# Projecting queries and keys together with the values, and turning them on VectorE and through DRAM

## The chip, the cores and the metric

The kernel runs on one core of a Trainium2 chip. The metric is the device time of one execution in microseconds (us). TensorE (PE) multiplies matrices; its weight loads have a row of their own in the profile (PEld). VectorE (DVE) and ScalarE (ACT) work on tiles element by element, GpSimd (POOL) and SyncE (SP) mostly issue transfers here. Matrix products land in PSUM, eight banks of 512 fp32 numbers on each of 128 partitions; everything else on the chip lies in SBUF.

## The reference

The input x has 4 images of 64 channels and 96 x 96 positions. Two layers follow one another, each on a group-normalized input and each added to what it got. The first is an attention with a sigmoid in place of a softmax; it takes nearly all of the time. The second filters a few frequencies of a 2-D Fourier transform.

```python
def _L0_conv_ref(x, wq, bq, wk, bk, wv, bv, ca_w1, ca_w2):
    q = jnp.einsum('bchw,oc->bohw', x, wq) + bq[None, :, None, None]   # 8 rows
    k = jnp.einsum('bchw,oc->bohw', x, wk) + bk[None, :, None, None]   # 8 rows
    v = jnp.einsum('bchw,oc->bohw', x, wv) + bv[None, :, None, None]   # 64 rows
    energy = jnp.einsum('bcn,bcm->bnm', Q, K)                          # 9216 x 9216
    att = jax.nn.sigmoid(energy)
    out = jnp.einsum('bcm,bnm->bcn', V, att).reshape(B, C, H, W) + x
    ...
    return out * scale[:, :, None, None]

x = x + _L0_conv_ref(_gn(x), ...)
x = x + _L1_conv_ref(_gn(x), ...)
```

## The kernel before

Two images make a pair and fill the 128 partitions; pair 0 runs through the attention first, then pair 1. The 9216 queries of a pair are cut into 18 blocks of 512, its keys into 72 pieces of 128. A tile is the product of 128 keys of one image with the 512 queries of a block: 144 tiles for each block of a pair, 5184 in all.

Tiles are worked in bursts of up to seven, one PSUM bank each. The eighth bank holds the block's sum (the accumulator, bank 7 or bank 0 by turns). In a burst, `energies` (L481) makes the tiles, with keys as the stationary and queries as the moving operand; `sigmoids` (L500) turns them into `at` in two ACT instructions, one over the first HEAD = 3 banks and one over the rest; `attend` (L517) multiplies values with `at` of the burst before and adds to the accumulator. While ACT works on burst t + 1, TensorE attends burst t. Queries and keys have 8 rows for each image. They are held four times over, as high and low parts of the fp32 numbers, so that a product over 32 rows of the faster fp32r form gives the accuracy of fp32.

Projections are steps between these. `keys` (L423 to L432) projects 512 positions with two matmuls of 256 columns; VectorE then adds the bias (L406), rounds to the high part (L407) and forms the low or high part (L416) in `kT`. `values_of` (L434 to L445) takes eight matmuls of 128 columns (L439), with x stationary, and one VectorE evacuation (L443) into `vT`. `queries` (L447 to L463) takes two matmuls of 256 columns (L452) and then eight VectorE instructions (L406, L407, twice L416, four times L462).

The order on TensorE, ACT and VectorE is written out by a planning loop (L671 to L737). It fills `together` (steps of a burst that use a bank of the next burst once the sigmoid has read it), `alone` (a step that takes the place of a tile: such a burst has six), and `ends` (work on VectorE or transfers after a burst). `done` (L733) says up to where a burst attends. A burst whose attention runs into the next block is a crossing; at the crossing the accumulator changes banks. During pair 0's first block its 18 pieces of keys and values are made just ahead of their use; pair 1's replace them while pair 0's last block runs. Queries of a block are made AHEAD = 42 tiles before it. In pair 1's time the second layer of pair 0 runs in the gaps. `halves` (L401) and `low_or_high` (L414) are the helpers of the splits.

The transfers on SP and POOL keep the order that the framework's scheduler gives them; each waits for what it needs, and holds up those behind it on its own queue.

Of the kernel before, what the change touches and what calls it, by code (L numbers as in the profile page):

```python
# [53 lines left out]

SIZE, HEAD = 7, 3
AHEAD = 6 * SIZE
ALL = NPAIR * NBLK * TILES
# [12 lines left out]

FIRST = {"wq": P, "wk": P, "wv": P, "pav": P, "bq": 1, "bk": 1, "low": 2, "nhalf": 1, "bv": P}
SECOND = {"w1": 2 * R, "w2": P, "ident": P, "fw": 2 * KW, "fh": 4 * KH, "gh": 2 * H, "gw": 4 * W}
# [11 lines left out]
def tile_kernel(ctx: ExitStack, tc: tile.TileContext, x, cst, late, spec, out):  # L84
# [299 lines left out]
    with tc.tile_pool(name="work", bufs=1) as work, \  # L384
# [10 lines left out]

        kT = kvp.tile([P, NCH // 2, P], F32R, tag="kT", name="kT")

# [3 lines left out]
        def halves(src, bias, name):  # L401

            shape = [P, src.shape[-1]]
            u = qp.tile(shape, F32, tag="full", name=f"full_{name}", bufs=1)
            h = qp.tile(shape, F32R, tag="high", name=f"high_{name}")
            nc.vector.tensor_scalar(u, src, bias, None, ALU.add)  # L406
            nc.vector.tensor_copy(h, u)  # L407
            return u, h
# [14 lines left out]
        def keys(p, s):  # L423
            pp = bank_a(f"pk_{p}_{s}")
            src = xs[p][:, bass.ts(s, NB)].rearrange("p (a e m) -> p e a m", e=2, m=P)
            for e in range(2):
                cols = bass.ts(e, P // 2)
                projected[0] = nc.tensor.matmul(pp[cols, :NB // 2], named("wk")[:, cols],  # L428
                                                src[:, e, :, :], start=True, stop=True)
            ku, kh = halves(pp[:, :NB // 2], named("bk"), f"k_{p}_{s}")  # L430
            low_or_high(kT[:, 2 * s:2 * s + 2, :].rearrange("p a m -> p (a m)"), ku, kh,
                        low_sb[:, 1:2])  # L432

        def values_of(p, s):  # L434
            pp = bank_a(f"pv_{p}_{s}")

            for i in range(4):
                for e in range(2):
                    projected[0] = nc.tensor.matmul(  # L439
                        pp[bass.ts(e, P // 2), bass.ts(i, P)],  # L440
                        xs[p][:, bass.ts(2 * (4 * s + i) + e, P // 2)], named("wv"),
                        start=True, stop=True)
            nc.vector.tensor_tensor(  # L443
                vT[:, 4 * s:4 * s + 4, :], pp.rearrange("p (i m) -> p i m", m=P),
                named("bv").unsqueeze(1).to_broadcast([P, 4, P]), ALU.add)  # L445

        def queries(p, n):  # L447
            pq = bank_a(f"pq_{p}_{n}")
            half = NB // 2
            for e in range(2):  # L450
                rows = bass.ts(e, P // 2)
                projected[0] = nc.tensor.matmul(  # L452
                    pq[rows, :half], named("wq")[:, rows],
                    xs[p][:, n * NB + e * half:n * NB + (e + 1) * half], start=True, stop=True)
            qu, qh = halves(pq[:, :half], named("bq"), f"q_{p}_{n}")
            q = qp.tile([P, NB], F32R, tag="q", name=f"q_{p}_{n}")
            for e in range(2):
                rows, cols = bass.ts(e, P // 2), bass.ts(e, half)
                low_or_high(q[rows, cols], qu[rows, :], qh[rows, :], low_sb[rows, 0:1])
                for b in range(2):  # L460
                    to, of = 64 * (1 - e) + 32 * b, 64 * e + 32 * b
                    nc.vector.tensor_copy(q[to:to + 32, cols], q[of:of + 32, cols])  # L462
            return q  # L463
# [13 lines left out]
        def energies(t):  # L477

            for i in range(total[t] - sizes[t], total[t]):
                r = 32 * (i % 4)  # L480
                nc.tensor.matmul(banks[:, bank_of(i), :], kT[r:r + 32, i // 4 % (NCH // 2), :],  # L481
                                 ask[i // TILES][r:r + 32, :], start=True, stop=True)
# [4 lines left out]
        def parts(t):  # L487

            for lo, part in ((0, order[t][:HEAD]), (HEAD, order[t][HEAD:])):
                if part:  # L490
                    yield 7 * (t % 2) + lo, min(part), len(part)
# [93 lines left out]
        norm0[0]()  # L585
        norm0[1]()
        keys(0, 0)
        warm_behind()
        q = first_queries()
        warm_behind()  # L590
        values_of(0, 0)
        warm_behind()
# [74 lines left out]
        kept = [TILES * (NPAIR * NBLK - 1) + 2 * (STRIP // P) * (s + 1) for s in range(NSTRIP)]  # L667
        ask, asked, known, valued, renewed, again_at = {0: q}, 1, 2, 2, 0, 0
        sizes, total, order, done, block, edges = [6], [6], [list(range(1, 7))], [], [], set()
        way = 1  # L670
        while len(done) < len(sizes):  # L671

            t, was = len(done), done[-1] if done else 0
            n = max(1, -(-was // TILES))
            edge = TILES * n
            crossing = edge < ALL and edge < total[t] - 3
            block.append(n if crossing else n - 1)
# [12 lines left out]
            elif total[t] < ALL:  # L690
                steps = together.setdefault(t, [])
                while known < NBLK and known <= (total[t] + 2 * SIZE - 1) // 8:
                    steps.append(lambda s=known: keys(0, s))
                    if known + 1 < NBLK:
                        end(t, norm0[known + 1])
                    known += 1
                while valued < NBLK and valued <= (total[t] + 2 * SIZE - LAG) // 8:
                    steps.append(lambda s=valued: values_of(0, s))
                    valued += 1
                if renewed < NBLK and was >= TILES * (NBLK - 1) + 8 * (renewed + 1):  # L700
                    steps.append(lambda s=renewed: keys(1, s))
                    steps.append(lambda s=renewed: values_of(1, s))
                    renewed += 1
                if asked < NPAIR * NBLK and total[t] + AHEAD >= TILES * asked and t not in alone:
                    steps.append(lambda n=asked: ask.update({n: queries(n // NBLK, n % NBLK)}))
                    asked += 1
                assert len(steps) <= HEAD
                while chain and not steps and t not in alone:
                    own, step, wait, since = chain[0]
                    if t < max(ready[0] + wait, started[0] + since):  # L710
                        break
                    if own:
                        alone[t] = step
                    elif own is None:
                        end(t, step)
                    else:
                        steps.append(step)
                    ready[0] = t
                    chain.pop(0)
# [6 lines left out]
            if crossing:  # L726
                way = 1 if n % 2 else -1
            elif together.get(t - 1):
                way = -way
            order.append(list(free)[::way][:ALL - total[t]])  # L730
            sizes.append(len(order[-1]))
            total.append(total[t] + sizes[-1])
            done.append(total[-1] - LAG if crossing else min(edge, total[-1] - LAG))  # L733
            while again_at < NSTRIP and done[t] >= kept[again_at]:
# [9 lines left out]

        spare[0] = 0
        energies(0)
        sigmoids(0)
        later(norm0[2])
        keys(0, 1)
        warm_behind()  # L750
        values_of(0, 1)
        with tc.manual_schedule(engines=ENGINES):
            put_off = []
            for t in range(T):
# [9 lines left out]
                if t + 1 < T:  # L764
                    sigmoids(t + 1)
                at_work = next((i for i in range(old, len(items)) if sum(
                    c.stop - c.start for _, c in items[:i]) >= 2 * NB), len(items))
                attend(items[old:at_work])
                for i, step in enumerate(together.get(t, ())):
                    spare[0] = order[t + 1][i]  # L770
                    step()
# [192 lines left out]
def _constants(l0):  # L964
# [19 lines left out]
    for name, w, bias in (("wq", "wq", "bq"), ("wk", "wk", "bk")):  # L984
        for col in range(P):
            b, o = col // 32 % 2, col % C8
            a[b * C:(b + 1) * C, PLACE[name].start + col] = l0[w][o]
            a[col, PLACE[bias].start] = l0[bias][o]
    for b in range(2):
        rows = slice(b * C, (b + 1) * C)  # L990
        a[rows, PLACE["wv"].start + b * C:PLACE["wv"].start + (b + 1) * C] = l0["wv"].T
        a[rows, PLACE["w1"].start + b * R:PLACE["w1"].start + (b + 1) * R] = l0["ca_w1"].T
        a[b * R:(b + 1) * R, PLACE["w2"].start + b * C:PLACE["w2"].start + (b + 1) * C] = \
# [3 lines left out]

    put("low", -np.stack([row // 8 % 2, row // 16 % 2], 1))
    put("nhalf", -0.5)
# [47 lines left out]
```

## Time and profile before

| What | Value |
|---|---|
| Median of three runs | 3080.54 us (3079.90 to 3081.23) |
| The profiled execution | 3080.95 us, span of its instructions 3079.2 us |
| First energies | 26.4 us after the span's start |
| Last energies | 2989.1 us |
| Attention, L517 | 11824 matmul records, 2408.3 us busy |
| Energies, L481 (all blocks but the first) | 5040 matmuls, 544.7 us busy |
| Sigmoids, L500 | 1503 instructions, 2394.5 us busy |
| Values' projection, L439 | 576 records, 37.7 us busy |
| Keys' projection, L428 | 144 records, 22.3 us busy |
| Queries' projection, L452 | 140 records, 21.1 us busy |
| DMA in the attention of pair 0 | about 1 GB/s |

A matmul in fp32 leaves two records, one in the fp32r form one. Matmuls are pipelined and two or four of them run side by side in parts of the array, so that busy times of single records overlap; the time between the starts of the same line in successive bursts is the better measure of a burst. The chain of waits goes back from the last instruction to whatever released each one, and gives the share of the span that each line holds.

### The profile page before, as it was taken

The numbers are of one execution on the slowest core, as the hardware profiler recorded it, in microseconds if no ns is written. First come the engines' busy times: TensorE is split into PE (matmuls) and PEld (weight loads), VectorE is DVE, ScalarE is ACT, GpSimd is POOL, SyncE is SP. The second block draws the span as 40 slices with busy tenths as digits, with TensorE's granted clock in tenths as the row PEclk, the third lists the DMA queues.
The fourth block names the chain that finished last, engine by engine and source line by source line (L and its number), as shares of the span: only waits on it lengthen the run. The fifth ranks groups of instructions, "written<-read, shape, count | busy, mean of one in ns | idle before, by whom it ended". The sixth has DMA issues, their size and how long they took to land.

```text
span 3079.2 us, 42720 instructions
## 1 busy us (share of the span) xinstructions
PE 3055.0 (99%) x19022; PEld 1145.5 (37%) x19022; DVE 387.2 (13%) x818; ACT 2417.3 (79%) x1543; POOL 27.1 (1%) x52
## 2 busy tenths in 40 slices
PE   8999999999999999999999999999999999999998
PEld 4433333333333333334433333333333333333336
DVE  4300000000000000002312111100110000000005
ACT  4688888888888888887688887777777888888872
POOL 0000000000000000000000000000001000000001
PEclk9999999999999999999999999999999999999999
DMA  3000000000000000000122322412113000000027
GB/s 145 1 1 1 1 1 1 1 1 1 1 1 1 1 1 1 1 1 1 31 75 61 84 74 77 132 24 29 50 44 131 1 1 1 1 1 1 5 63 246
DMA packets 80490, 99.48 MB, mean 32 GB/s; under 512 B 48209, under 2 KB 58193, under 8 KB 80209
## 3 DMA queue, kind: packets, MB, share of 16 engines
q1 hardware_dynamic: 72000, 71.57, 8.0%
q0 software_dynamic: 5776, 20.45, 1.9%
q10 hardware_dynamic: 2528, 4.72, 0.4%
q8 instruction: 149, 2.44, 0.3%
q14 instruction: 37, 0.29, 0.0%
HBM read 67.49 MB, written 28.05 MB: 31 GB/s over the span
## 4 chain that ended last, share of the span: by engine, by line
PE 98%; DVE 1%; ACT 1%; DMA 0%; issue 0%; SPq 0%; DVEq 0%; ACTq 0%
PE banks L517 75%; PE banks L481 16%; PE banks L439 1%; PE banks L428 1%; PE banks L206 1%; PE banks L376 1%; ACT at L500 0%; PE banks L452 0%; PE py L955 0%; PE pv L206 0%; DMA x<-in_x_dram 0%; PE pa L857 0%; PE banks L354 0%; PE idle_I-15036_15051 L820 0%; PE pu L869 0%
## 5 line engine op out<-in xcount | busy, mean ns | idle before, releaser
L500 ACT ACTIVATE at<-banks 128x1536 f32<-128x1536 f32 x1503 | 2394.5, 1640 | 590.6 <-PE banks L481 564.3
L517 PE MATMUL banks<-at,vT 128*64 128x512 f32 (+1 forms) x11824 | 2408.3, 546 | 0.0
L517 PEld LDWEIGHTS banks<-at,vT 128*64 128x64 f32 x11824 | 780.3, 136 | 1338.6 <-issue 1280.1
L481 PE MATMUL banks<-q,kT 32*128 32x512 f32 x5040 | 544.7, 453 | 2.6 <-ACT at L500 2.5
L481 PEld LDWEIGHTS banks<-q,kT 32*128 32x128 f32 x5040 | 223.6, 183 | 453.8 <-ACT at L500 340.0
L406 DVE TENSOR_SCALAR full_q<-banks,cs 128x256 f32<-128x256 f32 x35 | 16.9, 483 | 1361.0 <-PE banks L452 1361.0
L523 DVE SCALAR_TENSOR_TENSOR x<-banks,x 128x512 f32<-128x512 f32 x36 | 24.9, 692 | 648.9 <-PE banks L517 648.9
L462 DVE CAST q<-q 32x256 fp32r<-32x256 f32 x140 | 39.9, 285 | 3.8
L439 PE MATMUL banks<-cs,x 128*64 128x128 f32 x576 | 37.7, 273 | 0.4 <-DVE at L471 0.4
L379 DVE TENSOR_TENSOR x<-banks,x 128x384 f32<-128x384 f32 x24 | 13.4, 558 | 188.0 <-PE banks L376 186.1
L439 PEld LDWEIGHTS banks<-cs,x 128*64 128x64 f32 x576 | 33.8, 137 | 7.3 <-issue 0.9
L416 DVE SCALAR_TENSOR_TENSOR q<-high_q,cs,full_q 64x256 fp32r<-64x256 f32 x70 | 33.6, 480 | 1.8
L406 DVE TENSOR_SCALAR full_k<-banks,cs 128x256 f32<-128x256 f32 x36 | 17.4, 484 | 115.6 <-PE banks L428 89.8
L443 DVE TENSOR_TENSOR vT<-banks,cs 128x512 f32<-128x512 f32 x36 | 24.7, 685 | 9.7 <-PE banks L439 9.7
L525 DVE TENSOR_REDUCE maxs<-x 128x1 f32<-128x512 f32 x36 | 24.7, 686 | 1.2
L619 DVE COPY ws<-banks 128x512 f32<-128x512 f32 x16 | 11.1, 692 | 95.7 <-PE banks L206 95.6
L531 DVE BATCH_NORM_STATS2 stats<-x 128x6 f32<-128x512 f32 x36 | 22.2, 680 | 6.0 <-DMA x<-in_x_dram 5.8
L428 PE MATMUL banks<-x,cs 128*64 128x256 f32 x144 | 22.3, 388 | 0.2 <-DVE x L152 0.2
L570 PE MATMUL banks<-x 128*128 128x256 f32 (+1 forms) x46 | 14.9, 470 | 6.3 <-DMA x<-in_x_dram 6.3
L452 PE MATMUL banks<-x,cs 128*64 128x256 f32 x140 | 21.1, 379 | 0.0
L481 PE MATMUL banks<-q_first,kT 32*128 32x512 f32 x144 | 17.1, 463 | 2.8 <-DVE kT L416 1.7
L376 PE MATMUL banks<-cs,ws 128*64 128x384 f32 x96 | 19.6, 486 | 0.0
(133 smaller groups left out, 467.8 us busy)
## 6 DMA issues: line engine op xcount, KB each, us to landing
ws<-in_spec_dram SPq DMA_DIRECT2D x20, 512.0 KB
x<-in_x_dram SPq DMA_DIRECT2D x14, 512.0 KB
room<-in_spec_dram SPq DMA_DIRECT2D x12, 512.0 KB
w<-in_spec_dram POOLq DMA_DIRECT2D x10, 512.0 KB, 6.8
old<-in_x_dram SPq DMA_DIRECT2D x12, 384.0 KB
x1d<-x SPq DMA_DIRECT2D x12, 384.0 KB
xd<-old SPq DMA_DIRECT2D x12, 384.0 KB
xT<-xd SPq DMA_DIRECT2D x36, 128.0 KB
```

Source lines behind the costliest of these rows:

```text
L206: self.last = nc.tensor.matmul(pv[bass.ts(g, 32), :].rearrange("q (n k o) -> q n k o", n=SIDE, o=C)[:, :, k, :], self.ut[:, at:at + 32], s ...
L376: nc.tensor.matmul(py[bass.ts(b, C), :4 * W], self.z[:, i, bass.ts(b, C)], named("gw"), start=True, stop=True)
L406: nc.vector.tensor_scalar(u, src, bias, None, ALU.add)
L416: mark[0] = nc.vector.scalar_tensor_tensor(dst, h.bitcast(F32), is_low, u, ALU.mult, ALU.add)
L428: projected[0] = nc.tensor.matmul(pp[cols, :NB // 2], named("wk")[:, cols], src[:, e, :, :], start=True, stop=True)
L439: projected[0] = nc.tensor.matmul(pp[bass.ts(e, P // 2), bass.ts(i, P)], xs[p][:, bass.ts(2 * (4 * s + i) + e, P // 2)], named("wv"), star ...
L443: nc.vector.tensor_tensor(vT[:, 4 * s:4 * s + 4, :], pp.rearrange("p (i m) -> p i m", m=P), named("bv").unsqueeze(1).to_broadcast([P, 4, P ...
L462: nc.vector.tensor_copy(q[to:to + 32, cols], q[of:of + 32, cols])
L481: nc.tensor.matmul(banks[:, bank_of(i), :], kT[r:r + 32, i // 4 % (NCH // 2), :], ask[i // TILES][r:r + 32, :], start=True, stop=True)
L500: nc.scalar.activation(at[:, of:of + n, :], banks[:, bank:bank + n, :], AF.Sigmoid)
L517: attended[0] = nc.tensor.matmul(acc[half, cols], vT[:, j, half], at[:, place(2 * pair + b), cols], start=(j == 0), stop=(j == NCH - 1 and ...
L523: nc.vector.scalar_tensor_tensor(blk, acc, 1.0, blk, ALU.mult, ALU.add, accum_out=sums[p][:, m:m + 1])
```

## The change

Queries and keys lose their own projections, but for the first pieces. The values' weights get 32 more columns (16 for each image of the pair: 8 of the queries, 8 of the keys), so `values_of` makes all three, transposed, over two PSUM banks. VectorE adds the biases, splits queries and keys into high and low parts while they have positions on partitions, and turns them with one transpose. Four transfers on SP write the result to a DRAM tensor `split`, 32 rows of the three kinds for each piece. From there `known_keys` reads a piece of keys with four transfers on POOL, and `queries` a block of queries with eight transfers on SP, each of whole rows of 512 numbers.

Keys of pair 0's first seven pieces are still projected directly (DIRECT = 7), as are the first block's queries. The values of the very first piece keep the width of 128.

The transpose leaves the positions of a piece in another order. Stationary operands are therefore read with a step of two numbers: x in the values' projection, and `kT` in `energies`. The pieces of `vT` follow in the same order.

The planner changes too. Values are made further ahead (four bursts' tiles instead of two, less the lag). A values step takes two banks, so a burst's head, which ACT reads first, grows where steps need more than three. The first burst has five tiles instead of six. The rule for `crossing` and `done` is new. Reads of queries go into `ends` and no longer take a step. The three projections ahead of the first burst get banks of their own.

```diff
+QK = 4 * C8
+DIRECT = 7
...
-            src = xs[p][:, bass.ts(s, NB)].rearrange("p (a e m) -> p e a m", e=2, m=P)
             for e in range(2):
                 cols = bass.ts(e, P // 2)
-                projected[0] = nc.tensor.matmul(pp[cols, :NB // 2], named("wk")[:, cols],
-                                                src[:, e, :, :], start=True, stop=True)
+                projected[0] = nc.tensor.matmul(
+                    pp[cols, :NB // 2], named("wk")[:, cols],
+                    xs[p][:, bass.ts(2 * s + e, NB // 2)], start=True, stop=True)
...
+        def values_of(p, s, width=P + QK):
+            pp = banks[:, spare[0]:spare[0] + 2, :2 * width].rearrange(
+                "p h (a m) -> p h a m", a=2)
+            src = xs[p][:, bass.ts(s, NB)].rearrange("p (a m h) -> p a h m", a=2, h=2)
+            for h in range(2):
+                for a in range(2):
+                    for e in range(2):
+                        projected[0] = nc.tensor.matmul(
+                            pp[bass.ts(e, P // 2), h, a, :], src[:, a, h, bass.ts(e, P // 2)],
+                            named("wv")[:, :width], start=True, stop=True)
...
+            u = qp.tile([P, 2, 2, QK], F32, tag="u", name=f"u_{p}_{s}", bufs=1)
+            t = qp.tile([P, 3, 2, 2, QK], F32R, tag="t", name=f"t_{p}_{s}", bufs=1)
             nc.vector.tensor_tensor(
+                u, pp[:, :, :, P:].rearrange("p h a m -> p a h m"),
+                named("bqk").unsqueeze(1).unsqueeze(1).to_broadcast([P, 2, 2, QK]), ALU.add)
+            values()
...
+            for whole, to in pieces:
+                nc.vector.tensor_copy(to[:, 0], whole)
+                nc.vector.tensor_tensor(to[:, 1], whole, to[:, 0].bitcast(F32), ALU.subtract)
+            turned = qp.tile([P, 3, 2, NB // 8], F32, tag="turned", name=f"turned_{p}_{s}")
+            nc.vector.transpose(turned.rearrange("p k a (m h) -> p (k a) h m", h=2),
+                                t.rearrange("p k a h m -> p (k a) h m").bitcast(F32))
+            for g in range(4):
+                nc.sync.dma_start(
+                    split[p][s].rearrange("r k (a g m) -> g r (k a) m", a=2, g=4)[g],
+                    turned[bass.ts(g, QK)].rearrange("r k a m -> r (k a) m"))
+
+        def known_keys(p, s):
+            for r in range(4):
+                nc.gpsimd.dma_start(
+                    kT[bass.ts(r, QK), s, :].bitcast(F32),
+                    split[p][s][:, r % 2, bass.ts(r // 2, NB // 2)])
 
         def queries(p, n):
...
             q = qp.tile([P, NB], F32R, tag="q", name=f"q_{p}_{n}")
+            for i in range(8):
+                nc.sync.dma_start(
+                    q[bass.ts(i, QK // 2), :].bitcast(F32),
+                    split[p][n][bass.ts(i // 2 % 2, QK // 2), 2, :])
             return q
...
-                nc.tensor.matmul(banks[:, bank_of(i), :], kT[r:r + 32, i // 4 % (NCH // 2), :],
+                nc.tensor.matmul(banks[:, bank_of(i), :],
+                                 kT[r:r + 32, i % TILES // 8, :].rearrange(
+                                     "r (m h) -> r h m", h=2)[:, i // 4 % 2],
                                  ask[i // TILES][r:r + 32, :], start=True, stop=True)
...
-            crossing = edge < ALL and edge < total[t] - 3
+            crossing = edge < min(ALL, total[t] - 1)
...
-                while known < NBLK and known <= (total[t] + 2 * SIZE - 1) // 8:
-                    steps.append(lambda s=known: keys(0, s))
+                if known < DIRECT and known <= (total[t] + 2 * SIZE - 1) // 8:
+                    steps.append((1, lambda s=known: keys(0, s)))
                     known += 1
-                while valued < NBLK and valued <= (total[t] + 2 * SIZE - LAG) // 8:
-                    steps.append(lambda s=valued: values_of(0, s))
+                while (valued < min(NBLK, (total[t] + 4 * SIZE - 1) // 8 + 1)
+                       and sum(n for n, _ in steps) <= 2):
+                    steps.append((2, lambda s=valued: values_of(0, s)))
+                    if valued >= DIRECT:
+                        end(t, lambda s=valued: known_keys(0, s))
                     valued += 1
...
                 if renewed < NBLK and was >= TILES * (NBLK - 1) + 8 * (renewed + 1):
-                    steps.append(lambda s=renewed: keys(1, s))
-                    steps.append(lambda s=renewed: values_of(1, s))
+                    steps.append((2, lambda s=renewed: values_of(1, s)))
+                    end(t, lambda s=renewed: known_keys(1, s))
                     renewed += 1
-                if asked < NPAIR * NBLK and total[t] + AHEAD >= TILES * asked and t not in alone:
-                    steps.append(lambda n=asked: ask.update({n: queries(n // NBLK, n % NBLK)}))
+                if asked < NPAIR * NBLK and total[t] + AHEAD >= TILES * asked:
+                    end(t, lambda n=asked: ask.update({n: queries(n // NBLK, n % NBLK)}))
                     asked += 1
...
-            done.append(total[-1] - LAG if crossing else min(edge, total[-1] - LAG))
+            to = was + sizes[-1]
+            if to > total[t] - to % 2:
+                to = max(total[-1] - LAG, min(to, total[t] - total[t] % 2))
+            done.append(max(edge + 2, to) if crossing else min(edge, to))
...
-        spare[0] = 0
         energies(0)
         sigmoids(0)
         later(norm0[2])
+        spare[0] = 7
         keys(0, 1)
-        warm_behind()
+        spare[0] = 0
         values_of(0, 1)
```

## The prediction

> **What bounds the kernel now.** I read the busy shares first, then the chain of waits, then the same chain in short windows, then the groups of instructions by shape.
>
> ```profile
> PE 3055.0 (99%) x19022; PEld 1145.5 (37%) x19022; DVE 387.2 (13%) x818; ACT 2417.3 (79%) x1543; POOL 27.1 (1%) x52
> PE banks L517 75%; PE banks L481 16%; PE banks L439 1%; PE banks L428 1%; PE banks L206 1%; PE banks L376 1%; ACT at L500 0%; PE banks L452 0%; PE py L955 0%; PE pv L206 0%; DMA x<-in_x_dram 0%; PE pa L857 0%; PE banks L354 0%; PE idle_I-15036_15051 L820 0%; PE pu L869 0%
> ```
>
> TensorE is 99% of the span and 98% of the chain. A busy share can hide stalls, so the windows decide (start, us, what):
>
> ```profile
> 345.66 0.67 PE banks L481 x7
> 346.33 2.30 PE banks L517 x12
> 348.62 0.43 PE banks L452 x4
> 349.06 0.86 PE banks L517 x4
> 349.92 0.67 PE banks L481 x6
> 350.58 3.16 PE banks L517 x16
> ...
> 1443.76 0.43 PE banks L428 x4
> 1444.19 0.87 PE banks L439 x16
> 1445.06 0.86 PE banks L517 x4
> 1445.92 0.86 PE banks L481 x5
> ```
>
> A plain burst of seven tiles is 0.67 of energies and 3.16 of attention, 3.82 us. The burst with queries is 0.67 + 2.30 + 0.43 + 0.86 = 4.26: the projection's 0.43 is added whole, nothing hides it. Keys add 0.43, values 0.87. The energies after such a burst took 0.86 instead of 0.67: VectorE had not emptied the values' bank, as it does the keys first. ScalarE needs 3.22 us of each burst, so it doesn't take over when TensorE sheds these additions. A second stall, where a block of 512 queries ends:
>
> ```profile
> 449.39 0.46 PE banks L481 x2
> ...
> 449.93 0.77 ACT at L500
> 450.69 0.58 issue
> 451.27 1.88 ACT at L500
> ```
>
> Here attention stopped at the block's end and all of the next burst's work belonged to the new block, whose sum's bank ScalarE was still reading; by starts of successive bursts, the pair took 2.96 + 4.94 us against 3.82 + 3.39 elsewhere.
>
> **What the skill says.** SBUF — State Buffer, Specifications: lines of 16 bytes, full bandwidth from two hits a line on. That bears on the new layout of kT and x, read as stationary operand with a step of two fp32, two hits a line. The trace agrees at the extremes: step 1 takes 183 ns, z at L955 with a step of 32 elements 306 ns, both 32x128:
>
> ```profile
> L481 PEld LDWEIGHTS banks<-q,kT 32*128 32x128 f32 x5040 | 223.6, 183 | 453.8 <-ACT at L500 340.0 <-issue 110.4 <-DVE x L165 0.8
> L955 PEld LDWEIGHTS py<-cs,z 32*128 32x128 f32 x192 | 14.2, 306 | 0.8 <-DVE z L943 0.8
> ```
>
> No run shows step two. The same page, SBUF: two separate sides, says that VectorE's two-port operations keep GpSimd from writing descriptors for DMAs issued there, which bears on the keys' reads; no run before shows such a collision. DMA: Bandwidth & Descriptors, Anatomy of one DMA, puts the fixed cost of a transfer at about 2 us; here small ones measured 2.5 to 2.9.
>
> **The change part by part.**
>
> *Queries' projection goes.* 35 times 0.43. One falls in the first block, laid out below; 34 x 0.431 = 14.7 us off the path. Their VectorE work (about 2.9 us each) lay beside TensorE and frees nothing. The eight reads on SP's queue are issued about a block ahead where the q buffer allows; SP's order puts each behind the release of that buffer and few waits. Even asked 42 tiles (six bursts, 23 us) ahead, eight issues of 0.33 to 0.45 and a landing of 2.6 take 6 us. Cost nothing; if SP were blocked longer than the cover, each block would wait.
>
> *Pair 1's keys go, values widen.* Eighteen bursts of keys and values alternate between 5.13 and 5.33 us, 1.39 above plain. Afterwards values have 160 moving columns instead of 128: 0.87 x 160/128 = 1.08 us, plus 0.07 where VectorE's evacuation runs long: 1.15. VectorE now takes the 128-wide queries and keys first (a fixed 0.18 and 1 ns an element, from 128x512 at 685 ns and 128x384 at 558 ns: 0.31), then values 0.69; the two banks are free 1.2 us after the last matmul, about when the next energies reach them. 18 x 0.24 = 4.3 us.
>
> *Block ends.* The rule for `done` now always lets an ending burst begin in the old block. Four pairs of bursts lose 0.69 and four 0.27 (7.475 against 7.21): 3.8 us.
>
> *The first block (31 bursts from the first energies).* Here the added waits sit. A widened projection takes VectorE 0.31 + 0.69, six splits of 64 elements at about 0.2 (a 128x1 subtraction takes 158 ns, and 64 more elements 0.07), a transpose of 384 at 0.55 (768 takes 945 ns), some 3.0 us with gaps; direct keys 1.3, a normalization 0.54. That is 4.9 of the 5.3 us of a burst with both, so it keeps up, but the burst with two values needs 7.1 in 6.3 and the start carries a backlog. Behind each chain on VectorE's queue wait the next keys, for which energies wait. I laid the bursts out one by one with these durations. The same sheet gives 165.9 us for the start of the 31st burst before, where the trace has 166.0. Afterwards:
> - Start: separate banks let the queries' projection go before the keys' evacuation: 0.35 sooner. Five tiles instead of six shorten the first interval to 2.9 (3.79 before), and cost 0.4 in the last burst.
> - Removed: 24.7 us of additions in bursts 1 to 20. Added: five keys with values at 1.51, one double at 2.16, nine values at 1.08, together 19.4.
> - New stalls: 1.6 us behind the second chain, 2.8 behind the double, as keys 5 come after two chains.
> - Keys of chunks 7 to 17 go through DRAM. Four writes of 0.45 issue each and 2.6 to land (a write issued on SP at 3044.59 was seen at 3047.07) are 4.1; four reads on POOL, 0.52 each with 2.6 to land, are 4.2. In all 8.3 us after the transpose. From transpose to need there are two bursts, 10.2 less a spill of 1.8 to 2.2, so 8.0; where no values fall in between 7 or 5.9. Four or five of the eleven come late by 0.4 to 1.3.
>
> ```profile
> vt<-vd POOLq DMA_DIRECT2D x4, 64.0 KB, 2.6
> 3044.85 0.50 POOL L222 DMA_DIRECT2D vd<-vm  x1 [2.92 <-ACT vm L121]
> 3045.59 2.05 POOL L244 DMA_DIRECT2D vt<-vd  x4 [0.24 <-issue]
> ```
>
> The sheet's sum is 3.4 us later than before; with 0.6 for GpSimd's lock, 4.0. At a round trip of 5 to 7 us it is 1 to 2 us earlier; each us above 8.3 adds about four, so 13 us would add 20. With no DMA of this form in the trace I keep both ends.
>
> *Stationary operands with step two.* 5,184 weight loads of kT. Below: nothing. Above: as z, 306 - 183 = 0.12 us on the first loads of each burst, as the second round hides behind the first; 751 x 0.12 = 90. A gain is excluded, as nothing reads less. I take nothing, because two hits a line are granted full rate.
>
> *Moved without cost.* Larger head parts of the sigmoid occur once. Attention has 732 half-wide pieces instead of 728. In pair 1, keys read back have over 100 tiles of slack.
>
> Sum: -14.7 - 4.3 - 3.8 + 4.0 + 0.4 = -18.4. The profiled execution took 3080.95 (span 3079.2, 1.75 around it), 0.4 above the median of 3080.54: 3062.6, so **3063**.
>
> **Rivals.**
> 1. *Round trip late.* Were the DRAM trip 12 to 13 us, block 0 would cost 20 more: 3082. For it: four unproven hops, 256-byte pieces, and VectorE beside POOL. Against: the landings shown are steady. The gain is then hidden by a new wait of TensorE for kT.
> 2. *Stepped weights are slow.* This ends on the slower side: 3063 + 90 = 3153, decided on each energies' loads; from 25 ns a burst (18.4 / 751) on the gain is gone. For it: z. Against: z's step leaves one hit a line.
> 3. *More is saved:* no stall in block 0, about 3055 or less.
>
> **How the numbers follow.** Forecast 0.66 (own range 3054 to 3072), late round trip 0.17 (3073 to 3095), slow weights 0.12 (3100 to 3155), more saved 0.05. A measurement of this kernel can tell about 0.2%, 6.2 us, from no change: faster is below 3074.4. It takes 0.66 + 0.05 and 0.03 of the late cases: 0.74; within, 0.11; slower, 0.03 + 0.12 = 0.15. The range 3054 to 3085 leaves out more saved, slow weights and 0.03.
>
> **What would show it.** The line of the queries' projection gone; 160-wide values near 1.08 us; energies' weight loads still at 183 ns and plain bursts at 3.82, else rival 2; in the first 130 us, waits of energies for kT or its DMA of a few us in sum, else rival 1; block ends without a wait for ScalarE. Waits for q at a block's start would prove the reads' cover wrong.

## The result, and the profile after

| | Before | After |
|---|---|---|
| Median of six runs | 3080.82 us (3079.90 to 3082.28) | 3069.55 us (3067.01 to 3073.72) |
| Ratio to before | | 0.9963, 95% interval 0.9950 to 0.9976 |
| Profiled execution (span) | 3080.95 us (3079.2) | 3069.26 us (3067.5) |
| Last energies start at | 2989.1 us | 2977.7 us |

The change makes the kernel 11.3 us faster, a gain that the interval tells from nothing. It was forecast at 18.4; the time lies inside the forecast's own range of 3054 to 3072, near its upper end. The profiled executions differ by 11.7, and the experiments below show where the rest went.

The page after, its busy shares and its chain of waits:

```profile
PE 3045.5 (99%) x18772; PEld 1152.3 (38%) x18772; DVE 313.2 (10%) x731; ACT 2418.7 (79%) x1543; POOL 84.4 (3%) x168
PE 97%; DVE 1%; DMA 1%; issue 0%; ACT 0%; SPq 0%; POOL 0%; DVEq 0%; POOLq 0%; ACTq 0%
```

TensorE is still the bound. Its weight loads went up although it has 250 matmul records fewer: from 1145.5 to 1152.3 us. VectorE lost 74 us and GpSimd gained 57, both beside TensorE. The line of the queries' projection is gone. The weight loads of the energies, from the groups by shape:

```profile
L512 PEld LDWEIGHTS banks<-q,kT 32*128 32x128 f32 x5040 | 239.0, 190 | 450.5 <-ACT at L534 332.2 <-issue 116.1 <-DVE t L471 0.4
```

They take 190 ns on average where the kernel before had 183. A plain burst, from the start of its energies to the start of the next ones, went from 3.822 to 3.829 us. All 7 to 8 ns lie in the energies (0.664 to 0.671 us at the median); the attention stayed at 3.158 in both. This is too little to see in one burst, but there are some 750.

A block's end after the change. Timeline of TensorE: start us, busy us, line, shapes, count:

```profile
208.96 0.88 PE L512 MATMUL banks<-q,kT 32*128 32x512 f32 x7
209.76 3.23 PE L551 MATMUL banks<-at,vT 128*64 128x512 f32 x16
212.92 0.74 PE L512 MATMUL banks<-q,kT 32*128 32x512 f32 x6
213.59 3.23 PE L551 MATMUL banks<-at,vT 128*64 128x256 f32 x16
216.75 0.74 PE L512 MATMUL banks<-q,kT 32*128 32x512 f32 x7
217.42 2.79 PE L551 MATMUL banks<-at,vT 128*64 128x512 f32 x12
220.14 0.99 PE L512 MATMUL banks<-q,kT 32*128 32x512 f32 x7
```

The seven energies at 208.96 are the first that use the new block's queries. Attention follows 0.80 us after their start, instead of 0.67. The six at 212.92 belong to the crossing burst. Two short bursts then bring TensorE ahead of ScalarE, and the energies at 220.14 take 0.93 to the next attention: they wait for a sigmoid. I call these three places the last, the crossing and the third burst.

The waits of TensorE from 20 to 130 us, which is the first block (us in total, times, longest):

```profile
PE banks L512 <- DVE vT L451: 2.4, 2, 1.6
PE banks L512 <- DMA kT<-qk: 0.7, 1, 0.7
PE banks L512 <- ACT at L534: 0.6, 1, 0.6
```

VectorE's backlog shows twice. The list has gaps between matmuls alone; keys that came late through DRAM show in the timeline in five places, mostly as seven energies that take longer than their usual 0.74 us:

```profile
69.37 1.10 PE L512 MATMUL banks<-q_first,kT 32*128 32x512 f32 x7
84.90 0.69 PE L512 MATMUL banks<-q_first,kT 32*128 32x512 f32 x2 [0.74 <-DMA kT<-qk]
99.64 1.56 PE L512 MATMUL banks<-q_first,kT 32*128 32x512 f32 x7
116.20 0.76 PE L512 MATMUL banks<-q_first,kT 32*128 32x512 f32 x2 [0.23 <-DVE t L472]
120.05 2.01 PE L512 MATMUL banks<-q_first,kT 32*128 32x512 f32 x7
```

By the landings recorded in the trace, the last keys that these need came at 69.8, 85.1, 100.6, 116.4 and 121.5 us, some 0.5 to 0.6 us before the energies were through. (The fourth line names a split on VectorE, whose output energies don't read.) The five bursts took 0.4, 1.4, 0.8, 1.0 and 1.3 us longer by this, 4.9 in sum. DMA issues from 26 to 130 us, with the median from issue to landing:

```profile
qk<-turned SPq DMA_DIRECT2D x68, 48.0 KB, 2.0
kT<-qk POOLq DMA_DIRECT2D x44, 32.0 KB, 2.1
```

### The profile page after: what moved, and what is told of

Read it like the earlier page. It is cut to its first block, busy times and chain, and to the rows that moved or that the text cites. A ratio compares the mean times of both kernels' runs of the same rounds, so it can differ in the third digit from the quotient of the medians.

```text
span 3067.5 us, 43100 instructions
## 1 busy us (share of the span) xinstructions
PE 3045.5 (99%) x18772; PEld 1152.3 (38%) x18772; DVE 313.2 (10%) x731; ACT 2418.7 (79%) x1543; POOL 84.4 (3%) x168
## 4 chain that ended last, share of the span: by engine, by line
PE 97%; DVE 1%; DMA 1%; issue 0%; ACT 0%; SPq 0%; POOL 0%; DVEq 0%; POOLq 0%; ACTq 0%
PE banks L551 75%; PE banks L512 17%; PE banks L446 1%; PE banks L209 1%; PE banks L379 1%; PE py L1003 0%; PE pv L209 0%; PE pa L905 0%; DMA x<-in_x_dram 0%; ACT at L534 0%; PE banks L357 0%; PE idle_I-15339_15354 L868 0%; SPq L477 0%; PE pu L917 0%; PE banks L305 0%
## 5 line engine op out<-in xcount | busy, mean ns | idle before, releaser
L512 PE MATMUL banks<-q,kT 32*128 32x512 f32 x5040 | 551.2, 458 | 0.5
L512 PEld LDWEIGHTS banks<-q,kT 32*128 32x128 f32 x5040 | 239.0, 190 | 450.5 <-ACT at L534 332.2
L484 POOL DMA_DIRECT2D kT<-qk x116 | 57.4, 502 | 943.2 <-DMA qk<-turned 892.3
L446 PE MATMUL banks<-cs,x 128*64 128x160 f32 (+1 forms) x576 | 45.4, 299 | 0.0
L472 DVE TENSOR_TENSOR t<-u,t 128x64 fp32r<-128x64 f32 x105 | 23.5, 226 | 3.5
L474 DVE STREAM_TRANSPOSE turned<-t 128x384 f32<-128x384 f32 x35 | 20.7, 590 | 1.2
```

The lines of the kernel that those rows point to most:

```text
L446: projected[0] = nc.tensor.matmul(pp[bass.ts(e, P // 2), h, a, :], src[:, a, h, bass.ts(e, P // 2)], named("wv")[:, :width], start=True, s ...
L472: nc.vector.tensor_tensor(to[:, 1], whole, to[:, 0].bitcast(F32), ALU.subtract)
L484: nc.gpsimd.dma_start(kT[bass.ts(r, QK), s, :].bitcast(F32), split[p][s][:, r % 2, bass.ts(r // 2, NB // 2)])
L512: nc.tensor.matmul(banks[:, bank_of(i), :], kT[r:r + 32, i % TILES // 8, :].rearrange("r (m h) -> r h m", h=2)[:, i // 4 % 2], ask[i // TI ...
```

## The experiments

Each is the changed kernel with one edit, unless said otherwise. Single profiles of these kernels reach their second burst anywhere from 28.3 to 31.4 us, so effects of 1 to 3 us are read from the bursts of the trace and not from the totals. "Lost" below is the time by which a burst exceeds its nominal time, 0.835 us and 0.427 for each tile that it attends, which fits the plain bursts before. The first block's own scatter is larger: in the changed kernel and the five runs that share its first block (four transfers, old rules, price of a step, order kept, order reversed earlier) it lost 26.8 to 30.5 us.

### Stationary operands without a step

```diff
-                                 kT[r:r + 32, i % TILES // 8, :].rearrange(
-                                     "r (m h) -> r h m", h=2)[:, i // 4 % 2],
+                                 kT[r:r + 32, i % TILES // 8, bass.ts(i // 4 % 2, P)],
...
-            src = xs[p][:, bass.ts(s, NB)].rearrange("p (a m h) -> p a h m", a=2, h=2)
+            src = xs[p][:, bass.ts(s, NB)].rearrange("p (a h m) -> p a h m", a=2, h=2)
...
-                    split[p][s].rearrange("r k (a g m) -> g r (k a) m", a=2, g=4)[g],
-                    turned[bass.ts(g, QK)].rearrange("r k a m -> r (k a) m"))
+                    split[p][s].rearrange("r k (a h g m) -> g r (k a h) m", a=2, h=2, g=4)[g],
+                    turned[bass.ts(g, QK)].rearrange("r k a (h m) -> r (k a h) m", h=2))
...
```

> Undoes the step of two in the stationary operands: chunks of 128 consecutive keys, so that kT and x are read with step one; the price is DRAM writes in 128-byte pieces instead of 256. Theory (the step costs): the energies' weight loads go from 190 ns back to 183, the plain burst from 3.829 to 3.822 us, and the kernel ends 4.4 to 6 us earlier than the changed one (558 plain bursts alone gave 4.4), near 3064. Rival (the step is free, and the 7 ns come from somewhere else, as the layout of kT or the transfers beside it): loads stay at 190, plain bursts at 3.829, time within 1 us of the changed kernel. If the smaller DRAM pieces matter, the first block is longer by 1 to 3 us.

Measured: 3066.24 us, 0.9954 of before (0.9942 to 0.9967); 3.3 us less than after the change by the medians. The profiled span is 3062.8 us, 4.7 less, and the bursts behind the first block are 5.5 us shorter in sum. The loads, from the groups by shape:

```profile
L512 PEld LDWEIGHTS banks<-q,kT 32*128 32x128 f32 x5040 | 228.1, 182 | 450.9 <-ACT at L533 338.8 <-issue 109.9 <-DVE t L471 0.4
```

They are back at 182 ns and the plain burst at 3.822. The theory holds. The first block shows no cost of the smaller pieces beyond the scatter: it lost 29.4 us, after the change 28.3.

### The price of a step

The blocks of pair 0 read kT with steps 1, 4, 8, 16 and 32, three blocks each.

```diff
+            step = {1: 1, 2: 4, 3: 8, 4: 16, 5: 32}.get((i // TILES + 2) // 3, 2)
...
+            at = i // 4 % 18
+            return kT[r:r + 32, :, :].rearrange("r n m -> r (n m)")[:, at:at + step * P].rearrange(
+                "r (m h) -> r h m", h=step)[:, 0]
...
```

> Measures the disputed cost by itself: blocks 1 to 3 of pair 0 read kT with step 1, blocks 4 to 6 with step 4, 7 to 9 with step 8, 10 to 12 with step 16, 13 to 15 with step 32, the others with step 2 as in the changed kernel. The energies of blocks 1 to 15 then pair the queries with other keys' columns than the reference does. Theory (cost by how the reads fall on lines): step 1 183 ns, step 2 190, steps of 4 and more well above 200, up to the 306 ns that z has with step 32, and each plain burst grows by the excess of one load. Rival (cost not from the step): all near 190. If loads cost as z, the plain burst is 3.94 us.

Measured in a single execution of 3099.61 us: the groups by shape in five windows inside these stretches, in the order of the steps:

```profile
L521 PEld LDWEIGHTS banks<-q,kT 32*128 32x128 f32 x251 | 11.4, 182 | 22.3 <-ACT at L542 17.4 <-issue 4.8
L521 PEld LDWEIGHTS banks<-q,kT 32*128 32x128 f32 x285 | 20.9, 290 | 25.1 <-ACT at L542 22.2 <-issue 2.8
L521 PEld LDWEIGHTS banks<-q,kT 32*128 32x128 f32 x284 | 23.0, 318 | 24.5 <-ACT at L542 22.1 <-issue 2.4
L521 PEld LDWEIGHTS banks<-q,kT 32*128 32x128 f32 x285 | 22.0, 303 | 24.6 <-ACT at L542 20.1 <-issue 4.4
L521 PEld LDWEIGHTS banks<-q,kT 32*128 32x128 f32 x285 | 21.8, 299 | 25.4 <-ACT at L542 22.1 <-issue 3.2
```

The jump lies between 2 and 4: 182, 190, then 290 to 318 without a further trend. The bursts' medians follow: 3.824, then 3.949, 3.960, 3.936 and 3.934 us. A step of four fp32 is one hit on each 16-byte line, so this agrees with the lines that the Trainium skill states in SBUF — State Buffer, Specifications. But two hits a line, said to be full bandwidth, cost 7 ns of 183 here, and the measurement decides.

### The old rules for block ends

```diff
-            crossing = edge < min(ALL, total[t] - 1)
+            crossing = edge < ALL and edge < total[t] - 3
...
-            to = was + sizes[-1]
-            if to > total[t] - to % 2:
-                to = max(total[-1] - LAG, min(to, total[t] - total[t] % 2))
-            done.append(max(edge + 2, to) if crossing else min(edge, to))
+            done.append(total[-1] - LAG if crossing else min(edge, total[-1] - LAG))
```

> The changed kernel with the rules of before for when a burst crosses into the next block and how far attention has come after it. By the prediction's step this costs 3.8 us (8 pairs of bursts, four by 0.69 and four by 0.27), so 3073. Theory from the trace: the new rule won 2.7 us in the crossing bursts, but the two short bursts bring TensorE ahead of ScalarE, and the third burst after the crossing waits about 0.2 us for the sigmoid in 20 blocks, 3.9 us where before had 1.6 near its block ends; so the old rules cost only 0 to 1.5 us, and those waits are gone.

Measured: 3073.80 us, 0.9974 of before (0.9965 to 0.9984). My reading of the trace was wrong, and the prediction's term was nearer: the new rule is worth 4.3 us by the medians. The same block end, timeline of TensorE:

```profile
213.89 0.74 PE L512 MATMUL banks<-q,kT 32*128 32x512 f32 x7
214.57 2.37 PE L551 MATMUL banks<-at,vT 128*64 128x256 f32 x12
217.78 0.74 PE L512 MATMUL banks<-q,kT 32*128 32x512 f32 x6 [0.84 <-ACT at L534]
218.44 3.65 PE L551 MATMUL banks<-at,vT 128*64 128x512 f32 x16
```

Attention stops at the block's end after twelve matmuls, and TensorE stands 0.84 us until ScalarE lets a bank go. Over all blocks the last bursts lost 9.2 us instead of 3.4, the third ones 2.5 instead of 4.1. Counted by bursts the rule saves about 5 us. It doesn't account for the 0.1 us that each block's end still loses.

### Queries in four transfers

```diff
-            for i in range(8):
+            for i in range(4):
+                of = split[p][n][bass.ts(i % 2, QK // 2), 2, :]
                 nc.sync.dma_start(
-                    q[bass.ts(i, QK // 2), :].bitcast(F32),
-                    split[p][n][bass.ts(i // 2 % 2, QK // 2), 2, :])
+                    q[bass.ts(i, QK), :].bitcast(F32),
+                    bass.AP(tensor=of.tensor, offset=of.offset,
+                            ap=[[0, 2], [3 * NB, QK // 2], [1, NB]]))
```

> Reads the queries of a block back in 4 transfers instead of 8 (each lays 16 rows on 32 partitions). Theory: the plain burst before a block's end costs 0.115 us too much because the first energies of the new block wait one after the other for the semaphores of eight transfers that have long landed; with half of them about half of it goes, 29 to 35 times 0.05 to 0.06, 1.5 to 2 us earlier in all. Rival (those energies wait for ScalarE or for data): that burst stays at 3.94 us and the time unchanged.

Measured: 3069.09 us, 0.9959 of before (0.9946 to 0.9971), no different from the changed kernel. The trace shows half of the theory. The first energies of a new block have their 0.67 us again, in place of 0.72 to 0.84 at many block ends. But the last bursts still lost 2.7 us instead of 3.4: what came free went to another wait. After the last attention TensorE now took up to 0.28 us to the next energies, which is 0.17 elsewhere. They wait for ScalarE, and that pointed to the order of the banks.

### The order through the banks kept

A burst goes through its banks upwards or downwards (`way`). A step with a bank of its own reverses this. A crossing sets it to the block's own order, upwards and downwards by turns, which is a reversal where nothing has reversed it inside the block.

```diff
             if crossing:
-                way = 1 if n % 2 else -1
+                pass
             elif together.get(t - 1):
                 way = -way
```

> The changed kernel, but a burst that crosses into the next block keeps the order in which it goes through the banks instead of being set to the block's own. The trace of the run with four transfers left about 0.1 us in the last burst of every block: after its last attention TensorE takes 0.277 us to the next energies instead of 0.170, waiting for ScalarE. Theory: the order reverses there, so the first bank asked for is the one ScalarE reads last; before, the queries' projection reversed the order earlier in the block, under its own 0.43 us. Without the reversal the 0.107 goes at about 30 block ends, 3.2 us earlier, near 3066. Rival (the wait belongs to the six-tile burst or to the new block's queries): the 0.277 stays and the time is unchanged. A loss is possible where the bank of the old sum is now asked for first, before VectorE has read it: up to 0.7 us in 17 blocks.

Measured: 3069.23 us, 0.9967 of before (0.9955 to 0.9979), not told apart from the changed kernel; the trace has the answer. Another block end after the change, last and crossing burst, and below it the same one with the order kept:

```profile
1003.54 0.74 PE L512 MATMUL banks<-q,kT 32*128 32x512 f32 x7
1004.21 3.23 PE L551 MATMUL banks<-at,vT 128*64 128x512 f32 x16
1007.48 0.75 PE L512 MATMUL banks<-q,kT 32*128 32x512 f32 x6
```

```profile
1003.66 0.74 PE L512 MATMUL banks<-q,kT 32*128 32x512 f32 x7
1004.33 3.23 PE L551 MATMUL banks<-at,vT 128*64 128x512 f32 x16
1007.49 0.74 PE L512 MATMUL banks<-q,kT 32*128 32x512 f32 x6
```

From energies to energies 3.94 us against 3.83. The wait is the reversal: the first bank asked for is one that ScalarE reads last. Over all blocks the last bursts lost 1.7 us instead of 3.4. Where the block begins in another phase, the waits for eight semaphores remain.

### The order reversed earlier

```diff
...
-            elif together.get(t - 1):
+            elif together.get(t - 1) or t - 1 in asking:
```

> The changed kernel with the order through the banks reversed once more in the burst after the one that asks for queries, as the queries' projection did before. Theory: the block ends lose their 0.107 us, but a plain burst with nothing to hide the reversal pays it instead, so the sum stays within 1 us. Rival (a reversal is free inside a block): 3.2 us earlier.

Measured in a single execution: 3073.15 us, within the range of the changed kernel's own runs, so the total tells nothing. (The first energies came late in this run, its second burst at 31.4 us.) In its trace the last bursts again lost 1.7 instead of 3.4 us. Plain bursts away from the block ends lost about 2 us more than after the change, some 30 of them 0.06 us each. So a reversal isn't free inside a block; one costs less there than the 0.11 at a block's end, but what the ends gain is paid again in sum, as in the theory.

### Queries projected by TensorE

The queries' projection of before, in steps of one bank, everything else as changed.

```diff
+            pq = bank_a(f"pq_{p}_{n}")
+            half = NB // 2
+            for e in range(2):
+                rows = bass.ts(e, P // 2)
+                projected[0] = nc.tensor.matmul(
+                    pq[rows, :half], named("wq")[:, rows],
+                    xs[p][:, n * NB + e * half:n * NB + (e + 1) * half], start=True, stop=True)
...
```

> The changed kernel with queries projected by TensorE again, as before the change, in 34 bursts; the widened values and the keys by DRAM stay. By the prediction's first step this costs 34 times 0.431, 14.7 us. Theory: 3.2 to 4 us of that come back, since the projection reverses the bank order under its own time and the new block's energies wait for fewer semaphores: about 11 us later than the changed kernel, 3080. Rival (queries through DRAM brought nothing of the stalls at block ends): 14.7 later, 3084, with the waits in the last bursts of blocks unchanged.

Measured: 3083.52 us, 1.0010 of before (1.0001 to 1.0018), 14 us later than the changed kernel and by a hair slower than the one before. The last bursts of blocks lost 0.35 us instead of 3.4, about what the step of two costs them, so both waits there come with the queries' way through DRAM. The total is 3 us above the theory. In the profile two things that it left out add up to that: the first block lost 1.2 us more, which is within its scatter, and once, at 1503 us, energies stood 1.62 us for VectorE's split of queries. Without the queries' part, this change gains nothing.

### All keys of pair 0 projected by TensorE

```diff
-DIRECT = 7
+DIRECT = 18
```

> The changed kernel with the keys of all 18 chunks of pair 0 projected by TensorE, so that no energies of the first block wait for keys that go through DRAM. Theory (the DRAM trip is covered but for two chunks, and VectorE's chains are what hold the first block): eleven projections more on TensorE, 11 times 0.43 or 4.7 us, and 1.3 us more of VectorE for each, less the two DMA waits seen of 0.7 and 0.8: 3 to 8 us later than the changed kernel. Rival (the round trip costs the first block several us): no later, or earlier.

Measured in a single execution: 3073.45 us, within the range of the changed kernel's own runs. The first block lost 31.4 us instead of 28.3, and its waits for DMA are gone. But 1.7 of these 3 us are a longer stall of one attention in the sixth burst (5.1 us lost there instead of 3.4), which three runs with keys by DRAM have too (old rules, price of a step, direct queries). In the eighth to the nineteenth burst, where the two ways differ, direct keys lost 16.0 us; with keys by DRAM it was 14.8 after the change and 13.3 to 16.2 over nine profiles. So the DRAM trip costs the first block no more than it saves; that it saves anything isn't shown.

### Three edits together

> The changed kernel with three things at once: stationary operands without a step, queries read back in 4 transfers, and the order through the banks kept where a block ends. Theory: 4.6 us from the step (as measured alone), and at block ends the two waits that hid behind each other (the reversed order, 0.107 us at every end; the semaphores of eight transfers, 0.03 to 0.14 us at some of them) both go, 3.3 us in sum, where each alone gave 0.7 to 1.8. The last bursts of blocks then take 3.82 us, and the kernel ends near 3061.5. Rival (a third wait stands behind these): the last bursts stay above 3.87 us, and the kernel at 3064 or later.

Measured: 3061.48 us (3060.51 to 3062.55), 0.9936 of before (0.9922 to 0.9949): 8 us faster than the changed kernel and the best of all. The block end that was shown first, here:

```profile
208.81 0.73 PE L514 MATMUL banks<-q,kT 32*128 32x512 f32 x7
209.47 3.23 PE L552 MATMUL banks<-at,vT 128*64 128x512 f32 x16
212.63 0.73 PE L514 MATMUL banks<-q,kT 32*128 32x512 f32 x6
213.29 3.23 PE L552 MATMUL banks<-at,vT 128*64 128x256 f32 x16
216.53 0.74 PE L514 MATMUL banks<-q,kT 32*128 32x512 f32 x7
217.19 2.80 PE L552 MATMUL banks<-at,vT 128*64 128x512 f32 x12
219.92 0.99 PE L514 MATMUL banks<-q,kT 32*128 32x512 f32 x7
```

Its last burst takes 3.82 us, and all of them together lost 0.02. Each edit alone had uncovered the other's wait. How many semaphores the energies wait for can be counted in the events that TensorE's sequencer leaves at the energies' line, from 208 to 211.5 us, after the change and here:

```profile
L512 PEldq EVENT_SEMAPHORE  x4: 51/51/51, 209.0 to 209.8; - x4
```

```profile
L514 PEldq EVENT_SEMAPHORE  x1: 51/51/51, 209.5 to 209.5; - x1
```

No data is late there: in the changed kernel the eight reads of queries are issued as a block starts (from 209.5 us, 1.8 us to landing) and serve the block after it. The wait of the third bursts stays, 4.1 us in sum.

## Why the prediction came out as it did

The sum by its own terms, measured in the trace. The first block is the difference at the start of the 31st burst (166.0 and 166.8 us); the other rows are differences of lost time between the two profiles, with the 7.7 ns of the step taken out of each burst and put in a row of its own. How they are split between the rows is good to some 0.3 us:

| Term | Predicted | Measured |
|---|---|---|
| Queries' projection gone, pair 1's keys gone, values wider | -19.0 us | -19.7 |
| Block ends (and other plain bursts) | -3.8 | +1.0 |
| First block, with the start | +4.0 | +0.8 |
| Stationary operands with step two | 0 | +5.6 |
| Tile in the last burst, second layer, tail | +0.4 | +0.6 |
| Sum | -18.4 | -11.7 |

*Queries and pair 1* were right. The plain sum from the chain's 0.43 us a block held because nothing else became the bound. In the trace the 160-wide values took 1.09 us, forecast at 1.08. Direct queries cost 14 us when they were put back.

*Stepped operands* were taken at nothing "because two hits a line are granted full rate". This is the first of two mis-sized terms: 7.7 ns for each of about 720 bursts after the first block, 5.6 us; without the step the profile was 4.7 us shorter. The mechanism of rival 2 is real, at a sixteenth of its bound of 0.12 us. The bound itself was good: steps of four and more cost 0.11 to 0.14 us a burst.

*Block ends.* This is the second. The term for the rule stood: the crossing bursts lost some 3 us before and less than 0.5 after, and taken back the rule costs 4 to 5 us. What failed is the step on the queries' reads, "Cost nothing". It asked only whether the data come in time, and they do. But eight transfers bring several semaphores that the first energies wait for one after another. And the queries' projection had reversed the order of the banks beside its own 0.43 us; without it the reversal falls on the crossing, bare. Each costs about 0.1 us where it decides, 3.4 us in the last bursts, which had lost 1 us before. Further, the third bursts lost 4.1 us instead of 1.6: the time won at the crossing is partly given back there, as ScalarE is then late. With the old rules they lost 2.5, so the rule is a part of it; the rest is read from the waits alone. That, too, was left out of the 3.8. The sign that the prediction named, block ends without a wait for ScalarE, did not come.

*First block.* The forecast was nearly right about the late keys. From the transpose's end to the last landing, the round trip of the eleven pieces took 8.0 to 10.3 us, 8.8 in the median, where 8.3 was laid out. Writes landed in 2.0 us instead of 2.6, but their issues took 0.6 each instead of 0.45. Five pieces came late, by 0.4 to 1.4 us and 4.9 in sum; four or five were forecast, by 0.4 to 1.3. (The sheet's other lines come to -2.1 us, so that late keys had 5.5 in its sum of 3.4.) VectorE's two stalls were 0.8 and 1.6 us where 1.6 and 2.8 were laid out. Its pieces were no shorter than assumed, 2.79 us for one projection against 2.75 (bias 286 ns, three casts of 187 and three subtractions of 225, transpose 588, values 680). But they overlap, so that a chain took 2.6 us from start to end, not 3.0. The 0.6 for GpSimd's lock isn't seen apart: two of the reads of keys were issued 0.2 and 0.3 us behind the usual distance of 0.49, and what held them isn't shown. So the block was 3.2 us cheaper than forecast: about 2 at VectorE's stalls, 0.6 at the late keys, and the 0.6 of the lock. This is one profile. In the six that share this first block its end lay between 164.2 and 169.7 us, so the +0.8 is good to a few us at best.

Rival 1 is refuted: no trip took 12 us, and late keys cost 4.9 us, near the forecast. Rival 3 is out as well: stalls of 2.4 us for VectorE and 4.9 for keys are there in the first block. The errors of +5.6 and +4.8 on one side were partly covered by -3.2 and -0.7 on the other. That the time stayed inside the forecast's range is owed in part to this luck; the direction rested on the largest and best measured term. (The 3062.6 of the forecast counts from the profiled execution; from the median the sum gives 3062.1.)

## What to carry to other kernels

When a step is taken out of a tuned sequence, ask what else it did: here it reversed an order under its own time, and its data came with one engine's semaphore where eight transfers now bring their own. Count the transfers that feed one instruction, not only their landing, and multiply each nanosecond of a change in the innermost operand by the number of bursts. Two small waits at the same place hide each other: here removing one gave 0.7 us, the other 1.7, and both 3.4.

## What was not expected of the hardware

- A weight load of 32 x 128 fp32 numbers takes 182 ns with a step of one, 190 with two, and 290 to 318 with 4 to 32: a small cost at two, and no growth beyond four.
- Semaphores that were long satisfied still cost time: each event at the energies' line took 51 ns on TensorE's sequencer, and they spread the start of seven energies by 0.05 to 0.17 us.
- Transfers of 48 KB to DRAM landed 2.0 us after issue in the median, 0.6 us less than other small forms in the kernel before; issuing each on SP took about 0.6 us.
